# Preparing the next batch beside a batch's scan, and zeroing DRAM scratch beside the lookups

## The chip, the core and the metric

The kernel runs on one core of one Trainium2 chip. The metric is the time of one execution on the device in microseconds (us). A core has five engines that run their own instruction queues in order: TensorE (PE, matmuls, with its weight loads as PEld), VectorE (DVE), ScalarE (ACT), GpSimd (POOL), and SyncE (SP), which here only issues DMAs. POOL issues DMAs too. The on-chip memories are SBUF and PSUM; tables, partial sums and some intermediate results live in DRAM.

## What is computed

Four stages follow each other on an activation `x` of 4 batches x 512 tokens x 512 columns, each added to `x`:

```python
x = x + _L0_xattn_ref(_layernorm(x, axis=-1), fside_BxS2xS2_0, ctx_1024)
x = x + _L0_ffn_ref(_layernorm(x, axis=-1), L0_ffn_lut, L0_ffn_gate_idx, L0_ffn_up_idx, L0_ffn_down_idx)
x = x + _L1_xattn_ref(ctx_1024, _layernorm(x, axis=-1), L1_xattn_in_proj_w, L1_xattn_conv_w, ...)
x = x + _L1_ffn_ref(_layernorm(x, axis=-1), L1_ffn_gate_w, L1_ffn_w_gate, L1_ffn_w_up, L1_ffn_w_down)
```

The first is a pair of int8-quantized linears with a SiLU between them. The second is a gated FFN whose weights are looked up in a table of 16 values. The fourth is a mixture of 32 experts with the top 8 for each token. The change is about the third, a selective scan whose only link to `x` is the gate at its end:

```python
x = jnp.einsum('bld,ed->bel', hidden_states, in_proj_w)       # hidden_states is ctx_1024
xc = jax.lax.conv_general_dilated(x, conv_w, ...)             # 4 taps along the tokens
x = silu(xc + conv_b[None, :, None])                          # "u" in the kernel
x_dbl = jnp.einsum('bdl,ed->bel', x, x_proj_w)
dt_low, Bm, Cm = jnp.split(x_dbl, [dt_rank, dt_rank + d_state], axis=1)
dt = jax.nn.softplus(jnp.einsum('brl,dr->bdl', dt_low, dt_proj_w) + dt_proj_b[None, :, None])
...
state = state * jnp.exp(d[..., None] * A) + (d * u)[..., None] * b[:, None, :]   # for each token
y = jnp.einsum('bdn,bn->bd', state, c)
...
y = y + D[None, :, None] * x
y = y * silu(z)                                               # z is the layernorm of the running x
```

The convolution, the projection and the softplus need only the context, not the running `x`.

## The kernel before

The kernel is a list of Python generators. Each `yield` ends a step; `weave` interleaves the steps of several generators in proportion to weights, and that gives the order of the program. A scheduler then places the instructions on each engine's queue by that order and by when it reckons their inputs to be ready. Tiles come from pools; tiles with one tag share `bufs` buffers, so a new tile waits for the users of an old one.

- **Lookups** (to about 325 us). `smooth_quant` of the four batches is woven with `lut_weights`, which turns 27 groups of indices into FFN weights. The index loads go through SP (line 320) into two buffers `ix`.
- **Set-up.** `scan_weights` (line 400) loads the scan's weights. `routing_constants` (line 614) makes the router's constants, and zeroes what the experts need in DRAM: the first row of the two tables of normalized rows `xln` (line 644), 16 slot tables (line 669) and two sums of 4.5 MB each (line 671), all through SP.
- **Per batch, `scan` (line 478).** First a preparation: the context `cT` is loaded (line 484), four matmul groups `pi` (line 489), a convolution of three VectorE steps each (line 500), a SiLU into `u`, the projection `px` (line 510), which goes to DRAM as `xdbl` and comes back spread as `BC`, then the softplus. Its four slices `pd` (line 527) are done in two halves of two: Abs (533), max (534), Exp (537), three VectorE steps (539 to 541), then Ln for both halves (544), an add (545) and a product with `u` on POOL (546). The results, `dt` and `dt*u`, go to DRAM as `dts` through SP (line 549).
- Then the **scan proper**: 64 units a batch. Each loads 8 rows of `dts`, repeated 16 times over the partitions (512 KB, line 561), into half of a `pair` buffer. There are three pairs, and they share their tag with the softplus tiles. ScalarE takes exp into a PSUM bank `st` of tag "d" (line 566), POOL multiplies by B (568), VectorE runs the recurrence (569) and multiplies by C (571), and TensorE sums the states of four units at a time (578).
- Woven with the scan: the FFN of a batch, `lut_ffn`, 28 steps, and, from the second batch on, `route` of the batch before. The **gate** of the batch before (line 593) stands ahead of them; it uses a layernorm of a whole batch in a buffer `sz`, and PSUM tag "d".
- **After the last scan**: its gate and route, woven with the first 8 experts on the tokens of batches 0 and 1, and then all other expert work, which starts with reading the slot tables back.

PSUM in this part has tag "t" with 2 banks (transposes, the FFN's output, the router), "m" with 2 (FFN hidden), "y" with 1 (scan output) and "d" with 3.

Of the kernel before, what the change touches and what calls it, by code (L numbers as in the profile page):

```python
# [16 lines left out]
F32 = mybir.dt.float32  # L17
# [10 lines left out]
P = 128  # L28
# [31 lines left out]
class Kernel:  # L60
# [339 lines left out]
    def scan_weights(self, mp):  # L400
# [20 lines left out]
        self.dts = self.dram.tile([NB, HID, 2, S], F32, name="dts")  # L421

# [55 lines left out]
    def scan(self, mp, b):  # L478


        nc, t = self.nc, self.t
        conv_b, dt_b, skip = (self.vecs[:, i, :] for i in range(3))
        cT = mp.tile([P, DC // P, S], F32, tag="BC", name="cT", bufs=1)
        nc.sync.dma_start(out=cT, in_=t["ctxT"][b].rearrange("(k p) l -> p k l", p=P))
        u = mp.tile([P, KH, S], F32, tag="u", name="u", bufs=1)
        for e in range(KH):
            pi = self.bank("d", "pi")
# [19 lines left out]
        px = self.bank("d", "px")  # L507
# [3 lines left out]
        xd = mp.tile([nx, S], F32, tag="sc", name="xd", bufs=6)  # L511
        nc.scalar.copy(xd, px[:nx, :])
        nc.sync.dma_start(out=self.xdbl[b].rearrange("g n l -> (g n) l"), in_=xd)

        BC = mp.tile([P, 2, S], F32, tag="BC", name="BC", bufs=1)
# [4 lines left out]

        dts = []
        lost_ = mp.tile([P, KH, S], F32, tag="sz", name="lost", bufs=1)
        for e in range(KH):
            pd = self.bank("d", "pd")
            nc.tensor.matmul(
                pd, lhsT=self.dt_w[:, e * P : (e + 1) * P], rhs=xd[:RANK, :], start=True, stop=True
            )
            if e % 2 == 0:  # L530
                dts.append(mp.tile([P, 2, 2, S], F32, tag="dts", name="dt", bufs=3))
            d = dts[-1][:, e % 2]
            nc.scalar.activation(d[:, 1, :], pd, AF.Abs, bias=dt_b[:, e : e + 1])
            nc.vector.tensor_scalar(d[:, 0, :], pd, dt_b[:, e : e + 1], 0.0, ALU.add, ALU.max)
        for h, d in enumerate(dts):
            dt, w = d[:, :, 0, :], d[:, :, 1, :]
            nc.scalar.activation(w, w, AF.Exp, scale=-1.0)
            lost = lost_[:, 2 * h : 2 * h + 2, :]
            nc.vector.tensor_scalar(lost, w, 1.0, -1.0, ALU.add, ALU.add)
            nc.vector.tensor_tensor(lost, w, lost, ALU.subtract)  # L540
            nc.vector.tensor_tensor(dt, dt, lost, ALU.add)
        for h, d in enumerate(dts):
            dt, w = d[:, :, 0, :], d[:, :, 1, :]
            nc.scalar.activation(w, w, AF.Ln, bias=1.0)
            nc.vector.tensor_tensor(dt, dt, w, ALU.add)
            nc.gpsimd.tensor_tensor(w, dt, u[:, 2 * h : 2 * h + 2, :], ALU.mult)
            for i in range(2):
                e = 2 * h + i
                nc.sync.dma_start(out=self.dts[b, e * P : (e + 1) * P], in_=d[:, i])

        yield
        for e in range(KH):
            py = self.bank("y", f"py{e}")
            for v in range(4):
                scs = []
                for j in range(4):
                    if j % 2 == 0:
                        pair = mp.tile([P, 2, 2, S], F32, tag="dts", name="pair", bufs=3)
                    r0 = e * P + 32 * j + CPT * v
                    d = pair[:, j % 2]  # L560
# [30 lines left out]
        self.scanned = u  # L591

    def gate(self, mp, b):
# [3 lines left out]
        sz = mp.tile([P, TPB, HID], F32, tag="sz", name="sz", bufs=1)  # L597
        self.layernorm(sz, xb, TPB)
        for e in range(KH):
            th = mp.tile([P, S], F32, tag="sc", name="th", bufs=6)  # L600
            nc.scalar.activation(th, sz[:, e, :], AF.Tanh, scale=0.5)
            nc.vector.scalar_tensor_tensor(sz[:, e, :], th, 1.0, sz[:, e, :], ALU.add, ALU.mult)
            y = self.scanned[:, e, :]
            nc.vector.scalar_tensor_tensor(y, sz[:, e, :], 0.5, y, ALU.mult, ALU.mult)
            pt = self.bank("d", "pt_y")
# [574 lines left out]
```

## Time and profile before

| What | us |
|---|---|
| Median of 3 runs | 2057.48 (2054.28 to 2057.83) |
| The profiled execution | 2077.79 |
| Its span, first to last instruction | 2075.9 |
| PE busy | 1699.9 (82%) |
| DVE busy | 1216.7 (59%) |
| POOL busy | 975.7 (47%) |
| ACT busy | 673.6 (32%) |

The shares are means over parts with different limits. Roughly: 0 to 325 us lookups and quantized linears; 325 to 430 set-up, preparation of batch 0 and half of its FFN; 430 to 1199 the four scans; then experts to the end, where PE is busy nearly all the time from 1400 to 2000. The table of stretches that the prediction shows gives for each stretch its length, the busy time of each engine with the number of instructions in brackets, the TensorE clock granted, the busy share of the DMA engines (1 is full) and the GB/s moved. A line of the list of waits reads: engine, instruction's output and line, what it waited for, total us, times, longest us. A line of the timeline reads: start and length in us, engine, line, operation, output and inputs, number of instructions merged, and in brackets the engine's idle time before with what ended it. "SPq" is SP's issue of a DMA, not its transfer.

### The profile page before, as it was taken

To read this page: it belongs to the slowest core of one execution; us is meant where nothing else is said; L and a number is where in the kernel's file an instruction comes from. 1 tells how busy PE (TensorE), PEld (TensorE's weight loads), DVE (VectorE), ACT (ScalarE), POOL (GpSimd) and SP (SyncE) were. 2 spreads that over 40 slices of the span, in tenths; PEclk is the share of its full clock that TensorE was granted. 3 is DMA by queue.
4 is the path that set the end of the run, shared out by engine and by line. 5 is a ranking of instruction groups with operands and counts; after the bars stand their busy time and mean duration, and the time that the engine had idled before them with its cause. 6 is when DMAs were issued, how large, how long until landed. Compare 5 with 4: busy or idle time off the path is not lost. (4 is left out here: it accounts for less than half of the span.)

```text
span 2075.9 us, 24233 instructions
## 1 busy us (share of the span) xinstructions
PE 1699.9 (82%) x8385; PEld 996.7 (48%) x8385; DVE 1216.7 (59%) x2098; ACT 673.6 (32%) x1291; POOL 975.7 (47%) x844
## 2 busy tenths in 40 slices
PE   4777768978688779877987578679999999999980
PEld 2444337454344445544554244355556556566540
DVE  6777753479998888989888753122232223233232
ACT  1554342323453335333533332112222222222210
POOL 3111011055516771687168836635555555655431
PEclk9999978989898989998999689879999999999995
DMA  8421105099929972997299976648888877887756
GB/s 263 118 100 56 62 19 210 33 236 237 215 104 252 250 179 94 248 257 178 73 246 241 248 191 148 132 124 184 178 173 183 183 179 158 187 167 159 149 127 181
DMA packets 193207, 348.94 MB, mean 168 GB/s; under 512 B 46210, under 2 KB 92770, under 8 KB 193076
## 3 DMA queue, kind: packets, MB, share of 16 engines
q1 hardware_dynamic: 151332, 262.97, 47.2%
q0 software_dynamic: 41744, 84.34, 22.0%
q8 instruction: 68, 1.11, 0.2%
q14 instruction: 63, 0.52, 0.1%
HBM read 278.12 MB, written 77.57 MB: 171 GB/s over the span
## 5 line engine op out<-in xcount | busy, mean ns | idle before, releaser
L925 PE MATMUL pg<-exT,egu 128*128 128x320 f32 (+1 forms) x1536 | 408.2, 423 | 17.9 <-DVE eh L943 6.1
L968 POOL DMA_INDIRECT sums<-ey,to x168 | 261.0, 1554 | 283.3 <-DMA sums<-ey,to 128.5
L568 POOL TENSOR_TENSOR dBu<-pair,BC 128x512 f32<-128x512 f32 x256 | 326.8, 1279 | 134.5 <-DMA pair<-dts 116.4
L925 PEld LDWEIGHTS pg<-exT,egu 128*128 128x128 f32 x1536 | 291.6, 193 | 140.0 <-issue 44.7
L569 DVE TENSOR_TENSOR_SCAN st<-st,dBu 128x512 f32<-128x512 f32 x256 | 312.3, 1225 | 61.0 <-POOL dBu L568 49.4
L566 ACT ACTIVATE st<-pair,A 128x512 f32<-128x512 f32 x256 | 176.3, 691 | 330.5 <-DMA pair<-dts 269.2
L372 PE MATMUL pgu<-xT,wg 128*128 128x256 f32 (+1 forms) x704 | 199.8, 427 | 36.8 <-DVE h L382 36.5
L900 POOL DMA_INDIRECT xg<-xln,tokens x168 | 162.0, 964 | 103.5 <-PE pt_g L913 39.0
L942 DVE SCALAR_TENSOR_TENSOR eh<-eh,pg 128x320 f32<-128x320 f32 (+5 forms) x144 | 61.1, 424 | 227.9 <-ACT eh L941 127.9
L372 PEld LDWEIGHTS pgu<-xT,wg 128*128 128x128 f32 (+1 forms) x704 | 140.8, 209 | 104.0 <-DVE h L382 57.9
L333 PE MATMUL pw<-oh,lut_t 128*32 128x344 bf16 (+1 forms) x2052 | 131.3, 376 | 71.7 <-DVE oh L327 71.5
L372 PE MATMUL pgu<-xT,wu 128*128 128x256 f32 (+1 forms) x704 | 181.6, 398 | 0.0
L388 PE MATMUL po_f<-wd,h 128*128 128x512 f32 (+1 forms) x352 | 171.3, 631 | 12.1 <-DVE h L382 11.3
L954 PE MATMUL po_e<-ed,eh 128*128 128x512 f32 (+1 forms) x336 | 170.8, 628 | 12.0 <-DVE eh L943 4.1
L571 DVE TENSOR_TENSOR sc<-st,BC 128x512 f32<-128x512 f32 x256 | 169.0, 677 | 1.5
L965 DVE TENSOR_SCALAR ey<-po_e,gates 128x512 f32<-128x512 f32 x64 | 45.8, 747 | 210.4 <-PE po_e L958 127.5
L967 ACT ACTIVATE ey<-po_e,gates 128x512 f32<-128x512 f32 (+1 forms) x104 | 68.8, 684 | 285.4 <-PE po_e L958 140.3
L372 PEld LDWEIGHTS pgu<-xT,wu 128*128 128x128 f32 (+1 forms) x704 | 136.5, 198 | 40.5 <-issue 19.1
L578 PE MATMUL py<-sc,sum_states 128*32 128x512 f32 x512 | 80.7, 706 | 84.3 <-DVE sc L571 83.9
L796 POOL DMA_INDIRECT table<-i_tok,to x128 | 127.0, 992 | 38.9 <-issue 23.1
L333 PEld LDWEIGHTS <-lut_t 128*32 128x32 bf16 x2052 | 59.6, 105 | 124.8 <-issue 85.1
L388 PEld LDWEIGHTS po_f<-wd,h 128*128 128x128 f32 (+1 forms) x352 | 68.3, 201 | 98.8 <-issue 78.0
(266 smaller groups left out, 2011.1 us busy)
## 6 DMA issues: line engine op xcount, KB each, us to landing
pair<-dts SPq DMA_DIRECT2D x256, 512.0 KB
egu<-in_w_gate SPq DMA_DIRECT2D x40, 384.0 KB
ix<-idx_b SPq DMA_DIRECT2D x16, 688.0 KB
egu<-in_w_up SPq DMA_DIRECT2D x40, 256.0 KB
ed<-in_w_down SPq DMA_DIRECT2D x40, 256.0 KB
ed<-in_w_down SPq DMA_DIRECT2D x80, 128.0 KB
sums<-zero SPq DMA_DIRECT2D x2, 4608.0 KB
dts<-dt SPq DMA_DIRECT2D x16, 512.0 KB
```

The costliest lines, as they stand in the source:

```text
L333: nc.tensor.matmul(pt[i][32 * c : 32 * c + 32, :step], lhsT=self.lut_t[:, j, g, :], rhs=oh[:, c * n + i * step : c * n + (i + 1) * step], ...
L372: nc.tensor.matmul(pg[:m, j * W : (j + 1) * W], lhsT=w[:, k, c * P : c * P + m], rhs=xT[:, k, :], start=k == 0, stop=k == KH - 1,)
L388: nc.tensor.matmul(po, lhsT=h[:m, c, i * P : (i + 1) * P], rhs=self.wd[:m, c, :], start=c == 0, stop=c == NIC - 1,)
L566: nc.scalar.activation(st, d[:, 0, :], AF.Exp, scale=self.A[:, i : i + 1])
L568: nc.gpsimd.tensor_tensor(dBu, d[:, 1, :], BC[:, 0, :], ALU.mult)
L569: nc.vector.tensor_tensor_scan(st, st, dBu, 0.0, ALU.mult, ALU.add)
L571: nc.vector.tensor_tensor(sc, st, BC[:, 1, :], ALU.mult)
L796: scatter = nc.gpsimd.indirect_dma_start(out=tables[k % len(tables)], out_offset=bass.IndirectOffsetOnAxis(ap=to[:, i, k : k + 1], axis=0) ...
L900: nc.gpsimd.indirect_dma_start(out=xg[:m, :], out_offset=None, in_=xln, in_offset=bass.IndirectOffsetOnAxis(ap=tokens[:m, lo + j, col : co ...
L925: nc.tensor.matmul(pg[i][:, :hs], lhsT=w[:, k, i * P : (i + 1) * P], rhs=xT[:, k, z : z + hs], start=k == 0, stop=k == KH - 1,)
L954: nc.tensor.matmul(po[j][:m, :], lhsT=h[:, 0, b : b + m], rhs=wd[:, 0, :], start=True, stop=False)
L968: nc.gpsimd.indirect_dma_start(out=sums[j], out_offset=bass.IndirectOffsetOnAxis(ap=to[:m, lo + j, col : col + 1], axis=0), in_=y[:m, :], ...
```

## The change

It does the following.

- `scan` is split. `prepare` holds the convolution, the projection and the softplus, in nine steps; `scan` keeps the load of `BC` and the 64 units. `prepare` of batch 0 runs before the loop, woven with six FFN steps. `prepare` of batch b + 1 is woven with the scan of batch b. `u` gets two buffers.
- The softplus goes slice by slice, four times in a row, through one buffer `dt`: Abs, Relu, Exp and Ln on ScalarE. Its store to DRAM is issued by POOL instead of SP, and that of `xdbl` by ACT.
- The scan loads each unit into a tile `d` of its own, four buffers, in place of three pairs.
- The matmuls of the preparation and the gate's transposes use PSUM tag "t" in place of "d".
- The gate makes its layernorm row block by row block in scan buffers "sc". The router's `xn` has one buffer in place of two.
- Zeroing moves from `routing_constants` to a generator `scratch` that is woven with the lookups from step 36 on; each sum is zeroed by six stores in place of one, and every store is pinned behind what stands before it in SP's program. `routing_constants` comes after the first `prepare`.

```diff
-    def scan(self, mp, b):
+    def prepare(self, mp, b):
...
-        cT = mp.tile([P, DC // P, S], F32, tag="BC", name="cT", bufs=1)
+        cT = mp.tile([P, DC // P, S], F32, tag="c", name="cT", bufs=1)
...
-        u = mp.tile([P, KH, S], F32, tag="u", name="u", bufs=1)
+        u = self.u[b] = mp.tile([P, KH, S], F32, tag="u", name="u", bufs=2)
...
-            pi = self.bank("d", "pi")
+            pi = self.bank("t", "pi")
...
-        nc.sync.dma_start(out=self.xdbl[b].rearrange("g n l -> (g n) l"), in_=xd)
+        nc.scalar.dma_start(out=self.xdbl[b].rearrange("g n l -> (g n) l"), in_=xd)
+        yield
+        for e in range(KH):
+            pd = self.bank("t", "pd")
+            nc.tensor.matmul(
+                pd, lhsT=self.dt_w[:, e * P : (e + 1) * P], rhs=xd[:RANK, :], start=True, stop=True
+            )
+            d = mp.tile([P, 2, S], F32, tag="dt", name="dt", bufs=1)
+            dt, w = d[:, 0, :], d[:, 1, :]
+            nc.scalar.activation(w, pd, AF.Abs, bias=dt_b[:, e : e + 1])
+            nc.scalar.activation(dt, pd, AF.Relu, bias=dt_b[:, e : e + 1])
+            nc.scalar.activation(w, w, AF.Exp, scale=-1.0)
+            lost = mp.tile([P, DC // P, S], F32, tag="c", name="lost", bufs=1)[:, 0, :]
+            nc.vector.tensor_scalar(lost, w, 1.0, -1.0, ALU.add, ALU.add)
+            nc.vector.tensor_tensor(lost, w, lost, ALU.subtract)
+            nc.scalar.activation(w, w, AF.Ln, bias=1.0)
+            nc.vector.tensor_tensor(dt, dt, lost, ALU.add)
+            nc.vector.tensor_tensor(dt, dt, w, ALU.add)
+            nc.gpsimd.tensor_tensor(w, dt, u[:, e, :], ALU.mult)
+            nc.gpsimd.dma_start(out=self.dts[b, e * P : (e + 1) * P], in_=d)
+            yield
+
+    def scan(self, mp, b):
...
-                    if j % 2 == 0:
-                        pair = mp.tile([P, 2, 2, S], F32, tag="dts", name="pair", bufs=3)
...
-                    d = pair[:, j % 2]
+                    d = mp.tile([P, 2, S], F32, tag="d", name="d", bufs=4)
...
     def gate(self, mp, b):
...
-        sz = mp.tile([P, TPB, HID], F32, tag="sz", name="sz", bufs=1)
-        self.layernorm(sz, xb, TPB)
+        u = self.u[b]
         for e in range(KH):
...
+            sz = mp.tile([P, 1, S], F32, tag="sc", name="sz", bufs=6)
+            self.layernorm(sz, xb[:, e : e + 1, :], 1)
...
-            pt = self.bank("d", "pt_y")
+            pt = self.bank("t", "pt_y")
...
+    def scratch(self, c):
...
+        zero = c.tile([P, SLOTS], F32, name="zero")
+        nc.vector.memset(zero, 0.0)
...
+        yield from self.clear(zero, self.tables[0] + self.tables[1], SLOTS)
...
         for s in self.sums:
-            nc.sync.dma_start(
-                out=s.rearrange("(a p) d -> p a d", p=P),
-                in_=zero[:, :HID].unsqueeze(1).to_broadcast([P, NT + 2, HID]),
-            )
+            for a in range(0, NT + 2, 3):
+                z = nc.sync.dma_start(
+                    out=s.rearrange("(a p) d -> p a d", p=P)[:, a : a + 3, :],
+                    in_=zero[:, :HID].unsqueeze(1).to_broadcast([P, 3, HID]),
+                )
+                self.tc.keep_in_program_order(z)
+                yield
...
-            xn = rp.tile([P, 1, HID], F32, tag="xn", name="xn_r", bufs=2)
+            xn = rp.tile([P, 1, HID], F32, tag="xn", name="xn_r", bufs=1)
...
-                weave((sq, 30 * NB), (k.lut_weights(lp, k.jobs), 4 * len(k.jobs)))
+                lookups = k.lut_weights(lp, k.jobs)
+                weave((islice(sq, 40), 40), (islice(lookups, 36), 36))
+                weave((sq, 30 * NB - 40), (lookups, 4 * len(k.jobs) - 36), (k.scratch(lc), 4 * CHAINS))
...
+            weave((k.prepare(mp, 0), preps), (islice(ffn_, 6), 6))
             k.routing_constants(rp)
...
             for b in range(NB):
-                n = steps + (4 if b == 0 else 0)
+                n = steps - (2 if b == 0 else 0)
                 streams = [(k.scan(mp, b), units), (islice(ffn_, n), n)]
+                if b + 1 < NB:
+                    streams.append((k.prepare(mp, b + 1), preps))
```

## The prediction

> **What bounds the kernel now.** The cores view first: one core, span 2075.9 us; the profiled execution took 2077.8 us, 1.0% over the median of the runs, 2057.5 us. All sums below are made in that execution and carried to the median unchanged. Then the table of engine busy time by stretch. I cut it where the scan instruction (line 569) of each batch starts and stops; the same cut for that line alone gives 64 of them in each "scan" stretch and none in the four others.
>
> ```profile
> core 0: us, PE busy (x) PEld busy (x) DVE busy (x) ACT busy (x) POOL busy (x), PEclk, DMA share, GB/s
> 325.00:430.00 105.00, 99.60 (x350) 68.30 (x351) 44.69 (x106) 29.66 (x48) 9.79 (x18) 0.91 0.44 152
> 430.00:571.00 141.00, 104.42 (x408) 60.28 (x406) 129.98 (x170) 53.63 (x87) 82.20 (x68) 0.87 0.99 229
> 571.00:631.00 60.00, 52.33 (x186) 27.00 (x185) 54.06 (x117) 27.20 (x44) 11.13 (x10) 0.89 0.38 129
> 631.00:774.00 143.00, 111.77 (x457) 65.48 (x458) 127.87 (x171) 51.63 (x85) 112.54 (x98) 0.91 0.96 227
> 774.00:838.00 64.00, 61.28 (x232) 36.58 (x232) 54.16 (x126) 34.62 (x55) 11.99 (x11) 0.92 0.32 113
> 838.00:980.00 142.00, 109.98 (x448) 63.34 (x448) 130.29 (x171) 51.86 (x84) 112.41 (x98) 0.94 0.97 233
> 980.00:1046.00 66.00, 60.53 (x238) 37.14 (x239) 55.92 (x132) 35.12 (x56) 11.28 (x10) 0.92 0.30 98
> 1046.00:1199.00 153.00, 108.28 (x408) 57.88 (x406) 129.19 (x169) 50.84 (x90) 125.23 (x109) 0.84 1.04 245
> ```
>
> The reader should see two kinds of stretch. In a scan the 16 DMA engines are full (0.96 to 1.04): 64 loads in 141 us is 2.2 us a load. VectorE is then 84 to 92% busy. In a gap of 60 to 66 us the DMA falls to a third, yet VectorE stays at 85 to 90%. So a gap isn't empty: most of it is gate, routing, convolution and softplus on VectorE. Moving work out of a gap therefore doesn't save the gap; it saves the idle parts of VectorE, and no more. That is the main point of the forecast.
>
> Next the list of waits and the timeline, for where the idle time sits.
>
> ```profile
> ACT st L566 <- DMA pair<-dts: 269.2, 189, 12.4
> POOL dBu L568 <- DMA pair<-dts: 116.4, 132, 7.0
> ...
> 339.05 6.77 SPq L671 DMA_DIRECT2D sums<-zero  x2
> 345.86 11.53 SPq L484 DMA_DIRECT2D cT<-in_ctxT  x1
> ...
> 382.48 7.03 PE L489 MATMUL pi<-cT,in_w 128*128 128x512 f32 x16
> ...
> 417.46 5.39 SPq L549 DMA_DIRECT2D dts<-dt  x4
> ...
> 429.08 0.69 ACT L566 ACTIVATE st<-pair,A 128x512 f32<-128x512 f32 x1 [3.91 <-DMA pair<-dts]
> ...
> 628.98 0.69 ACT L566 ACTIVATE st<-pair,A 128x512 f32<-128x512 f32 x1 [12.39 <-DMA pair<-dts]
> ```
>
> ScalarE's wait for loads is the DMA bound of the scans. At the start, the load of batch 0's context stands behind 9 MB of zeros on SP's queue, its convolution begins at 382.5, and the scan at 430.5. TensorE isn't idle there: it runs half a batch of FFN first. And between two batches ScalarE waits 12.4 us for the first tile to go out to DRAM and come back; VectorE has other work for 9.8 of the 12 us from 620, so even this is mostly covered.
>
> **What the Trainium skill says.** "ScalarE: Activation LUTs", What ACT_TABLE_LOAD costs: a switch of set costs a 1283 ns load, and a drain as well. The trace has the load at 1283 ns: six at line 544 (Ln), and reloads for the next exp or tanh. "SBUF — State Buffer", SBUF: two separate sides: a DMA issued by GpSimd can wait for its descriptors while VectorE holds the shared port. The trace shows only a possible echo, line 546 on POOL taking 2341 to 3502 ns for one form. "DMA: Bandwidth & Descriptors", Issuing engines are not separate DMA queues: a store issued by GpSimd shares the same 16 engines, so moving it buys no bandwidth. No run here shows it; I charge the store its full slot.
>
> **The change part by part.**
>
> *Zeros.* 16 table and 12 sums stores move from 331-346 us into the lookups. DMA share there is 0.06 to 0.44 after the first 40 us, so 9.4 MB find room. SP is charged 7.4 + 1.4 us for tables and 6.8 us for sums, all behind or ahead of index loads, of which SP spends 136 us waiting for buffers. A store of 0.77 MB ahead of an index load delays it by about 3 us (at 260 GB/s); most of these have a spare buffer. Bounds: 0 to +10 us; taken +3.
>
> *Start of batch 0.* The scan weights are issued by 330.4, the context load follows and lands near 334. The old chain then gives: convolution matmul to u done 15 us (382.5 to 397.8), u to xd 2, first softplus slice Abs 0.7, Relu 0.7, Exp 0.6, two VectorE steps 1.1, table load and Ln 1.9, one add 0.7, POOL product about 1.5, so some 9 us with semaphores; then dts store to first scan 13 us (417.5 to 430.5), plus about 1 us because GpSimd issues it. 334 + 15 + 2 + 9 + 14 = 374; taken 376. Only the first of four slices stands before the scan; with one dt buffer the others follow at some 14 us each, and the scan needs one every 35 us. The scan starts 54 us earlier, but this isn't a saving of 54 us: of the 44.7 us of VectorE work before 430, about 25 come before 376 (FFN of six steps, convolution, one slice, constants), so 20 move behind it.
>
> *VectorE work from 376 to the end of scan 3.* From 430 to 1199 the table sums to 681.5 us. Add the 20. Take off the max at line 534 in three batches, 12 x 0.74 = 9, which becomes a ScalarE Relu. Add four layernorms of one row block for one of four (line 103 and 106, six more small ones a batch, 0.16 each) and four half-length softplus steps for two: about 4. Sum 697 us.
>
> *What it is divided by.* This is the choice that decides. The old mean from 430 to 1199 is 681.5/769 = 0.886. Its 88 us of idle time are 62 in the four scans (11, 15, 12 and 24: length less busy), where the DMA is last, and 26 in the three gaps (6, 10 and 10), where chains through other engines are. Only these can be won. After the change each load has 697/256 = 2.7 us of VectorE work beside it instead of 2.0, so the 2.2 us of DMA is no longer last; the whole DMA work of that stretch, shares times lengths, is 637 us, 84% of what follows. I take 0.92, the best that a scan stretch shows, since instructions are queued in a fixed order and other engines are not slack: TensorE has about 660 us of busy time in it. 697/0.92 = 758, end of scan 3 at 1134 instead of 1202: -68. At 0.886 the end is 1163 (-39), at 0.97 it is 1095 (-107).
>
> *Edits hidden at first sight.* ScalarE gets Relu 0.69 x 16 and single Exp and Ln calls; with exp of the scan between slices, each Ln costs two loads, 16 x 2.6 = 41 us against about 15 now. It is 44% busy, and three st banks hold 3 x 1.9 = 5.7 us of VectorE work, which covers a pause of 3.2 us; without that cover 12 slices x 3 = 36 us. The matmuls of the preparation and of the gate move from the three banks "d" to the two banks "t", beside po_f, which holds one for 10 us at a time; the price is TensorE waiting, with 10% to spare, 0 to +15, in the divisor. POOL gets 16 stores of about 0.7 us (as for line 304): +11 on 469, hidden. The d buffers fall from three pairs to four singles: see the slower rival.
>
> *Behind the last scan.* Gate and route of batch 3 sit on the chain to the late experts: TensorE is busy only half of 1330 to 1372. The layernorm of the gate can't all run before the scan ends, as it now borrows scan buffers: +5. The one routing buffer xn instead of two makes each layernorm wait for its store: 3 steps grow from 3 us to about 5: +5. Bounds +2 to +20; taken +10.
>
> Sum: -68 + 3 + 10 = -55 us; 2057.5 - 55 = 2002.5.
>
> **The rivals.**
>
> *A. More overlap.* VectorE at 0.97: -107 + 10 = -97, 1960 us. For it: it is fed by several independent streams. Against: no stretch of 50 us in the trace is above 0.95.
>
> *B. New waits eat the periods.* Every preparation step stops the ScalarE or TensorE queue for a bank, for the single dt buffer or for Ln, and exp of the scan waits behind it. At 0.86 and a tail of +25: 697/0.86 = 810, end 1186, -16 + 28 = +12 at worst, with the cover half there about 2045 us.
>
> *C. The four d buffers (slower).* Place: SP's loads at the d tile. With three pairs a load takes 10 us from issue to use, the first alone 6.2 us. A buffer is then held 1.4 us until POOL is done, so four of them give one load per (6.2 + 1.4)/4 = 1.9 us at best, under the 2.2 of the DMA. If stores of dts, xln and kept stretch a load's trip, the ring becomes the bound. It decides from a cycle of (1202 - 376 - 13)/256 = 3.2 us a load, a trip of 11.3 us. At 12.2 us it is 3.4 us a load: 376 + 870 + 13 = 1259, +57, 2114 us; nearer the point, 2080. For it: such trips of 15 to 20 us do occur at the end of scan 3, when expert weights load. Against: with fewer loads in flight the own queue is shorter.
>
> **How the numbers follow.** Forecast 0.60 (1975 to 2030), A 0.12, B 0.14 (0.10 faster, 0.03 same, 0.01 slower), C 0.14. About 0.2%, 4 us, can be told from no change. Faster 0.60 + 0.12 + 0.10 = 0.82, same 0.03, slower 0.15. The range takes the forecast with its bounds (divisor, tail, zeros), nearly all of A and the better half of B: 1953 to 2046; C is left out. The likeliest case's own range is 1975 to 2030.
>
> **What would show it.** First scan instruction near 376; no stretch without scans of over 15 us between batches; VectorE 90% or more and DMA near 0.85 from there to the last scan near 1134; ACT table loads up to about 40; the late experts (line 925) about 55 us earlier, from their first matmul to their end as long as before. Wrong if the first scan stays after 400, if VectorE is below 0.87 there, if loads take over 11 us from issue to use, or if the lookups end after 335.

## The result

The changed kernel takes 2083.23 us (median of 4 executions, 2079.09 to 2087.18). The ratio to the kernel before is 1.0121, with a 95% interval of 1.0090 to 1.0153: slower by 1.2%, where 2.7% faster was forecast. The time lies outside the range, and the sign is wrong. The profiled execution took 2087.18 us. That is only 9 us more than the 2077.79 us of the profile before, because that profile caught a long execution: over all later runs the kernel before took 2042.81 to 2077.45 us. So sizes below are taken from ratios (1% is 20.6 us), and places from the traces; differences of places from the kernel before carry that error too.

### The profile after

The same table of stretches, cut at the first scan instruction of each batch. The gaps of 60 us and more without scans are gone. The last line is a part of the second.

```profile
core 0: us, PE busy (x) PEld busy (x) DVE busy (x) ACT busy (x) POOL busy (x), PEclk, DMA share, GB/s
325.00:375.00 50.00, 44.12 (x159) 29.08 (x160) 24.98 (x63) 24.32 (x37) 4.11 (x8) 0.90 0.26 70
375.00:563.00 188.00, 152.29 (x555) 84.76 (x553) 162.09 (x225) 92.23 (x143) 99.28 (x86) 0.91 0.84 207
563.00:781.00 218.00, 180.83 (x682) 107.79 (x679) 187.62 (x309) 94.17 (x152) 133.20 (x119) 0.88 0.74 188
781.00:999.00 218.00, 178.62 (x700) 103.46 (x698) 189.51 (x308) 94.67 (x154) 132.58 (x120) 0.92 0.74 184
999.00:1186.00 187.00, 143.29 (x598) 87.73 (x598) 160.34 (x275) 60.37 (x106) 125.25 (x112) 0.89 0.84 203
...
375.00:435.00 60.00, 39.42 (x120) 21.36 (x119) 42.97 (x59) 28.25 (x44) 27.41 (x26) 0.80 0.71 179
```

The first scan instruction came as forecast: it stands at 375 instead of 430. But after four of them the scan stands still for 27 us, from 382.8 to 410.1, while the last two softplus slices of batch 0 go through ScalarE and VectorE; VectorE is busy for 43 of the 60 us to 435. Between the batches no more than 11 us pass without a scan instruction. The DMA share is down to 0.74 to 0.84, also as forecast. Yet from the start on the four periods take 811 us, where scans and gaps took 769 before. VectorE is busy for 700 of them, which is 0.863 of the time and not 0.92. The last scan ends at 1185, 13 us earlier than before, not 68.

The waits of the changed kernel from 375 to 1186 (waiting engine, line, what it waited for; total us, times, longest):

```profile
ACT st L561 <- DVE sc L566: 219.8, 110, 10.4
...
ACT st L561 <- DMA d<-dts: 43.9, 33, 5.0
POOL dBu L563 <- DMA d<-dts: 42.3, 44, 7.5
...
ACT dt L525 <- DMA dts<-dt: 36.7, 7, 7.5
...
DVE lost L529 <- ACT dt L527: 27.4, 8, 5.4
DVE ln_off L106 <- POOL ln_rs L104: 23.1, 17, 4.4
...
DVE st L564 <- POOL dBu L563: 22.6, 16, 5.1
...
DVE st L564 <- ACT st L561: 9.5, 2, 8.1
```

and one line of the kernel before:

```profile
DVE st L569 <- POOL dBu L568: 49.4, 58, 5.5
```

Before, ScalarE waited 269 us for loads. Now it waits 44 us for loads, and 220 us for VectorE to free a PSUM bank. VectorE is last, as the forecast wanted, and still stands idle for 111 us of the stretch (before: 87 of 768). The line for L525 is new: ScalarE stops before the next slice until the store has emptied the single dt buffer. The lines of DVE show what was won and what was lost. VectorE's waits for POOL's product, behind which the loads stand, fell from 49.4 to 22.6 us. In their place it waits 27.4 us for the Exp of a softplus slice (line 529) and 23.1 us for POOL in the layernorms (line 106; 4.6 us before).

Behind the last scan another 22 us went: the late experts start 193.6 us after it (1185.3 to 1378.9), where it was 171.4 us (1198.1 to 1369.5).

### The profile page after: what moved, and what is told of

Same layout as the page of the kernel before. It is cut to its first block, busy times and chain, and to the rows that moved or that the text cites. A ratio compares the mean times of both kernels' runs of the same rounds, so it can differ in the third digit from the quotient of the medians.

```text
span 2085.4 us, 24364 instructions
## 1 busy us (share of the span) xinstructions
PE 1703.8 (82%) x8385; PEld 1003.2 (48%) x8385; DVE 1218.4 (58%) x2138; ACT 707.8 (34%) x1343; POOL 999.5 (48%) x880
## 5 line engine op out<-in xcount | busy, mean ns | idle before, releaser
L563 POOL TENSOR_TENSOR dBu<-d,BC 128x512 f32<-128x512 f32 x256 | 337.3, 1324 | 221.8 <-DVE st L564 108.9
L564 DVE TENSOR_TENSOR_SCAN st<-st,dBu 128x512 f32<-128x512 f32 x256 | 303.7, 1213 | 33.7 <-POOL dBu L563 22.6
L561 ACT ACTIVATE st<-d,A 128x512 f32<-128x512 f32 x256 | 173.8, 689 | 269.2 <-DVE sc L566 219.8
L372 PE MATMUL pgu<-xT,wg 128*128 128x256 f32 (+1 forms) x704 | 195.2, 422 | 41.5 <-DVE h L382 41.5
L372 PE MATMUL pgu<-xT,wu 128*128 128x256 f32 (+1 forms) x704 | 175.9, 390 | 0.0
```

Source lines behind the costliest of these rows:

```text
L372: nc.tensor.matmul(pg[:m, j * W : (j + 1) * W], lhsT=w[:, k, c * P : c * P + m], rhs=xT[:, k, :], start=k == 0, stop=k == KH - 1,)
L561: nc.scalar.activation(st, d[:, 0, :], AF.Exp, scale=self.A[:, i : i + 1])
L563: nc.gpsimd.tensor_tensor(dBu, d[:, 1, :], BC[:, 0, :], ALU.mult)
L564: nc.vector.tensor_tensor_scan(st, st, dBu, 0.0, ALU.mult, ALU.add)
```

## The experiments

Ratios are to the kernel before, timed beside each run. "Last scan" and "late experts" (their first matmul) are read from each run's trace, one execution each. Not all rows were timed on the same chip, so they are compared by their ratios.

| Run | Median us | Ratio (95% interval) | Last scan ends | Late experts start |
|---|---|---|---|---|
| changed kernel | 2083.23 | 1.0121 (1.0090 to 1.0153) | 1185.3 | 1378.9 |
| block | 2116.99 | 1.0263 (1.0220 to 1.0306) | 1223.2 | 1416.4 |
| zeros | 2021.41 | 0.9796 (0.9755 to 0.9837) | 1144.4 | 1322.2 |
| split | 2064.40 | 1.0021 (0.9996 to 1.0045) | 1169.8 | 1359.5 |
| tail | 2058.23 | 0.9987 (0.9968 to 1.0005) | 1184.4 | 1356.6 |
| inline | 2075.71 | 1.0134 (1.0102 to 1.0165) | 1189.5 | 1381.3 |
| inline6 | 2071.15 | 1.0094 (1.0066 to 1.0123) | 1182.3 | 1377.6 |
| both | 2036.34 | 0.9928 (0.9907 to 0.9949) | 1170.8 | 1338.8 |
| noln | 2049.49 | 0.9982 (0.9966 to 0.9998) | 1161.7 | 1351.6 |
| zeros_slice | 2040.31 | 0.9877 (0.9839 to 0.9915) | 1156.5 | 1333.7 |
| gate | 2077.09 | 1.0077 (1.0053 to 1.0101) | 1175.8 | 1368.4 |
| best | 2020.95 | 0.9808 (0.9777 to 0.9839) | 1152.7 | 1322.9 |
| all | 2034.82 | 0.9870 (0.9839 to 0.9901) | 1163.3 | 1332.5 |
| all_noln | 2032.86 | 0.9856 (0.9827 to 0.9886) | 1136.7 | 1317.8 |
| zeros_noln | 2028.43 | 0.9823 (0.9792 to 0.9854) | 1146.8 | 1330.1 |
| pair | 2055.21 | 0.9945 (0.9925 to 0.9965) | 1164.0 | 1346.5 |
| zeros_half | 1980.82 | 0.9637 (0.9607 to 0.9666) | 1108.4 | 1290.3 |
| all_half | 1998.27 | 0.9721 (0.9693 to 0.9750) | 1128.6 | 1302.5 |

### First theory: the weave gains nothing, and the tail loses

**zeros** is the kernel before with its zeroing moved, as the change has it, and nothing else:

```diff
...
-                weave((sq, 30 * NB), (k.lut_weights(lp, k.jobs), 4 * len(k.jobs)))
+                lookups = k.lut_weights(lp, k.jobs)
+                weave((islice(sq, 40), 40), (islice(lookups, 36), 36))
+                weave((sq, 30 * NB - 40), (lookups, 4 * len(k.jobs) - 36), (k.scratch(lc), 4 * CHAINS))
```

> The kernel before with one part of the change alone: the zeros are stored beside the lookups. The context of batch 0 no longer waits behind them on SP's queue. Theory 1: scan 0 starts some 20 us earlier (430 to about 410), half of that is given back as VectorE work that moves behind the start, the last scan ends 8 to 15 us earlier, time 2040 to 2050. Rival (the start is worth nothing, since FFN and VectorE work of the same amount must still be done): within 4 us of the kernel before.

Faster by 2.0% (the two medians alone, 2021.41 and 2059.39, give 1.8%): more than twice what was expected, and the largest single effect of the study. Its stretch from its first scan to its last:

```profile
core 0: us, PE busy (x) PEld busy (x) DVE busy (x) ACT busy (x) POOL busy (x), PEclk, DMA share, GB/s
380.00:1144.50 764.50, 630.94 (x2498) 371.04 (x2496) 681.51 (x1061) 303.79 (x500) 459.70 (x395) 0.92 0.82 203
```

The first scan moves from 430 to 380 with the preparation where it was, and all of it arrives at the last scan (1144.4 for 1198.1); no stop as in the changed kernel follows the start. VectorE's work from the first scan on is 681.5 us, the same as before from 430 on. So the early start, which the forecast gave to the change as a whole, comes from the zeros alone. What is left of the change then costs 1.0121 / 0.9796 = 1.033, some 67 us.

**block** and **inline** put the preparation of batches 1 to 3 back between the scans, with all else as changed:

```diff
 block:
-                if b + 1 < NB:
-                    streams.append((k.prepare(mp, b + 1), preps))
                 if b:
+                    run(k.prepare(mp, b))
                     run(k.gate(mp, b - 1))
 inline:
-                streams = [(k.scan(mp, b), units), (islice(ffn_, n), n)]
-                if b + 1 < NB:
-                    streams.append((k.prepare(mp, b + 1), preps))
+                streams = [(chain(k.prepare(mp, b), k.scan(mp, b)) if b else k.scan(mp, b), units + (preps if b else 0)), (islice(ffn_, n), n)]
```

> The changed kernel, but the preparations of batches 1 to 3 stand as blocks between the scans again; the early start of batch 0, the zeros beside the lookups and all buffers stay. Theory 1 (the woven preparation gains nothing, because VectorE's queue, which runs in order, is stopped by its short chains as long as the gaps cost before): the last scan ends within 10 us of the changed kernel's 1185, time within 12 us of 2083. Rival (the weave does what the forecast said and the loss lies elsewhere): three gaps come back, last scan ends at 1210 or later, time 2105 to 2125.

> The changed kernel, but the preparation of batches 1 to 3 stands in front of its own scan in one stream, as in the kernel before, so that FFN and routing steps fill the gap (in run block they did not). All buffers, forms and banks of the change stay. Theory 2 (the forms that the weave needed, single buffers, slice by slice softplus, shared bank and short layernorms, cost the 40 us that the scans grew over run zeros; the weave itself gives nearly as much as it takes): as slow as the changed kernel, last scan ends at 1180 or later, time 2075 to 2095. Rival (the weave itself costs them, by chains put between scan units): back to run zeros in the scans, last scan near 1150, and with the tail's loss of 22 us a time of 2040 to 2052.

Block came out where its rival said, at 2117 us. But it undoes more than the weave: in its three gaps VectorE is busy for 28 of 42 to 46 us, since no FFN step fills them, and the scans beside which they stand instead take 185 to 191 us. It said little about the weave. Inline has the order of the kernel before, with FFN steps in the gaps, and is as slow as the changed kernel: 1.0134 and 1.0121, intervals that nearly coincide. So the weave is not where the time went. On the buffers and forms of the change it neither gains nor loses, to within the intervals; the loss is there without it, and comes with the buffers and forms that were changed to make room for it.

### Second theory: the forms cost, one by one

**tail** changes two things for batch 3 alone: where the gate's transposes go, and a second buffer for the router.

```diff
-            pt = self.bank("t", "pt_y")
+            pt = self.bank("d" if b == NB - 1 else "t", "pt_y")
...
-            xn = rp.tile([P, 1, HID], F32, tag="xn", name="xn_r", bufs=1)
+            pool, tag = (self.mp, "xd") if b == NB - 1 and i % 2 else (rp, "xn")
+            xn = pool.tile([P, 1, HID], F32, tag=tag, name="xn_r", bufs=1)
```

> The changed kernel with two edits that act behind the last scan only: the transposes of the gate of batch 3 use PSUM tag d (free by then) instead of t, and the router of batch 3 has a second buffer for its normalized rows. Theory 1 (the 22 us that the stretch from the last scan to the late experts grew come from these two): late experts 10 to 18 us earlier, time 2065 to 2073. Rival (they come from the expert instructions that stand ahead in ScalarE's and POOL's queues): under 5 us, 2078 to 2086.

1.3% faster, some 28 us, where 10 to 18 were expected. The scans end where they did (1184.4 and 1185.3), and the late experts start 22 us earlier. First the timeline of the changed kernel, gate and router of batch 3 (start, length, engine, line, in brackets the idle time before):

```profile
1190.47 1.11 PE L603 MATMUL pt_y<-ident,u 128*128 128x128 f32 x4 [2.05 <-DVE ln_rs L103]
...
1215.35 0.66 PE L603 MATMUL pt_y<-ident,u 128*128 128x128 f32 x4
...
1235.21 0.81 ACT L108 ACTIVATE xn_r<-x,ln_off,ln_rs 128x512 f32<-128x512 f32 x1 [0.70 <-DMA xln<-xn_r]
```

Then the same in run tail:

```profile
1196.00 0.60 PE L603 MATMUL pt_y<-ident,u 128*128 128x128 f32 x4
...
1201.56 0.63 PE L603 MATMUL pt_y<-ident,u 128*128 128x128 f32 x4 [1.15 <-DVE u L599]
...
1207.71 1.76 ACT L108 ACTIVATE xn_r<-x,ln_off,ln_rs 128x512 f32<-128x512 f32 x2 [6.90 <-DVE ln_off L106]
```

Four transposed tiles are spread over 25 us in the changed kernel, between transposes and outputs of the first experts that use the same two banks; in run tail they are through in 6 us. The router then makes two rows' layernorms back to back, where it waited for the store of the row before: its four layernorms start within 8 us, and took 19. The last logits come out at 1224.7 instead of 1244.8, and the scatters and the late experts move up with them. The two edits were not run apart. In the traces some 13 of the 20 us are won before the first of the router's layernorms, where the banks act, and some 6 after it, where the buffer does.

**split** cuts a softplus slice into three woven steps, **noln** leaves the logarithm out (Identity in its place):

```diff
 split:
             nc.scalar.activation(w, w, AF.Exp, scale=-1.0)
+            yield
             lost = mp.tile([P, DC // P, S], F32, tag="c", name="lost", bufs=1)[:, 0, :]
...
             nc.vector.tensor_tensor(dt, dt, lost, ALU.add)
+            yield
             nc.vector.tensor_tensor(dt, dt, w, ALU.add)
 noln:
-            nc.scalar.activation(w, w, AF.Ln, bias=1.0)
+            nc.scalar.activation(w, w, AF.Identity, bias=1.0)
```

> The changed kernel with each softplus slice cut into three steps instead of one (a step ends after the Exp and after the first add), so that its VectorE instructions are woven in later than the ScalarE instructions they wait for. Theory 1: VectorE's wait for the Exp (27 us, line 529) falls by half or more, its idle time between 375 and the end of the last scan falls from 111 us to about 95, the last scan ends 10 to 20 us earlier, time 2063 to 2073. Rival (the idle time only changes its name, the bound being elsewhere): the wait at the slice falls but the sum stays at 105 to 115, time 2078 to 2088.

> The changed kernel with the logarithm of the softplus left out: Identity in its place, which reads and writes the same tile in the same time and needs no other table. Theory of the table loads (16 slices at two loads of 1.28 us each stop ScalarE, and VectorE behind it): last scan ends 15 us or more earlier, time 2055 to 2068. Rival (ScalarE has slack, it waits 220 us for free banks anyway): within 6 us of 2083.

Both gained, split 1.0% and noln 1.4%, each a little more than its theory asked. The groups of the changed kernel show the table loads, with which ScalarE changes its set of functions (busy us, mean ns, then idle time before and what ended it):

```profile
L531 ACT ACT_TABLE_LOAD x16 | 20.5, 1283 | 9.8 <-DVE lost L530 8.6 <-DVE ln_rs L103 1.1
...
L380 ACT ACT_TABLE_LOAD x8 | 10.3, 1283 | 0.1
L561 ACT ACT_TABLE_LOAD x8 | 10.3, 1283 | 2.0 <-DMA d<-dts 1.9
```

From 375 to the last scan the changed kernel loads tables 28 times, run zeros 8 times, run noln never. Twenty loads more are 26 us of ScalarE. Of the 28, 14 stand in front of a slice's Ln, and 14 in front of the exp of the scan or the tanh of the FFN that follows it, as the timeline of the changed kernel shows for one slice, with two lines of the next slice at its end:

```profile
702.08 0.62 ACT L527 ACTIVATE dt<-dt 128x512 f32<-128x512 f32 x1
...
705.11 0.69 ACT L561 ACTIVATE st<-d,A 128x512 f32<-128x512 f32 x1 [1.82 <-DVE sc L566]
...
706.35 1.28 ACT L531 ACT_TABLE_LOAD   x1 [0.55 <-DVE lost L530]
...
706.79 2.20 DVE L532 TENSOR_TENSOR dt<-dt,lost 128x512 f32<-128x512 f32 x1
707.17 1.27 POOL L563 TENSOR_TENSOR dBu<-d,BC 128x512 f32<-128x512 f32 x1
707.64 0.63 ACT L531 ACTIVATE dt<-dt 128x512 f32<-128x512 f32 x1
708.29 1.28 ACT L380 ACT_TABLE_LOAD   x1
...
722.80 0.69 ACT L525 ACTIVATE dt<-pd,vecs 128x512 f32<-128x512 f32 x1 [7.52 <-DMA dts<-dt]
...
724.62 0.43 DVE L529 TENSOR_SCALAR lost<-dt 128x512 f32<-128x512 f32 x1 [5.44 <-ACT dt L527]
```

ScalarE waits for VectorE (the bank of line 561), VectorE's queue holds the slice's steps, and these wait for ScalarE (27.4 us at line 529). Two queues that run in order wait for each other by turns. In run split the slice's wait falls from 27.4 to 8.0 us and VectorE's idle time from 111 to 94; in run noln they fall to 8.7 and 88.

The last two lines show a second cause that no run took out by itself: the single dt buffer. Seven of the eight waits at line 529, 27.0 of the 27.4 us, come straight after ScalarE stood at line 525 until the store had emptied that buffer. This stand falls from 36.7 us to 7.2 in run split and 9.8 in run noln. So both runs may gain by way of the buffer, and a second dt buffer with all the loads in place was not tried: what the loads cost and what the buffer costs isn't told apart.

Split and noln remove largely the same time: with split in place (run all below, which has other edits too), leaving out the logarithm gains 0.1% in the ratio, within the intervals.

**both** is tail and split together, **gate** computes the statistics of the four row blocks at once, **inline6** gives run inline six load buffers instead of four (the room comes from the second u buffer):

```diff
 gate:
+        rs, off = self.statistics(xb, TPB)
         for e in range(KH):
             sz = mp.tile([P, 1, S], F32, tag="sc", name="sz", bufs=6)
-            self.layernorm(sz, xb[:, e : e + 1, :], 1)
+            self.normalize(sz, xb[:, e : e + 1, :], rs[:, e : e + 1], off[:, e : e + 1])
 inline6:
-                    d = mp.tile([P, 2, S], F32, tag="d", name="d", bufs=4)
+                    d = mp.tile([P, 2, S], F32, tag="d", name="d", bufs=6)
```

> Runs split and tail in one kernel. If the two losses stand in different stretches and add up, 19 + 25 us come off the changed kernel: 2035 to 2043. If the one was only the other's shadow (both end at the same later bound): 2052 to 2060. Either way the rest over run zeros, some 18 us, would be what weaving costs still.

> The changed kernel, but the gate computes the statistics of its four row blocks in one go (one power on POOL instead of four), and still normalizes block by block in the scan's buffers. Theory 2: four of VectorE's waits for POOL a batch become one, the waits of line 106 fall from 23 us to about 12, last scan some 8 us earlier, time 2068 to 2078. Rival (these waits stand where VectorE would wait for something else): within 4 us of the changed kernel, a ratio of 1.010 to 1.014.

> Run inline with one u buffer instead of two, as its order allows, and six d buffers in their room instead of four. Theory of the ring (four load buffers are too few once the scan runs alone beside the DMA): 15 us or more faster than run inline, the wait for d in ScalarE and POOL falls. Rival (the ring is not the bound): within 6 us of run inline.

Tail and split nearly add up (0.9928, with an interval from 0.9907; 1.0121 less 1.3% and 1.0% is 0.989). Gate gains 0.4%, with intervals that just overlap, and its last scan ends 9.5 us earlier, as expected, though its waits for POOL at the layernorms fell only from 23.1 to 19.3 us, where about 12 was expected. So the gate's form explains little of these waits. Inline6 gains 0.4% over inline, with intervals that overlap, half of what its theory asked: the ring of four, the slower rival of the prediction, is at most a small part.

**zeros_slice** is the cross-check from the other side: run zeros, and the slice-by-slice softplus alone, in the old place and with the old buffers.

```diff
-        for h, d in enumerate(dts):
-            dt, w = d[:, :, 0, :], d[:, :, 1, :]
-            nc.scalar.activation(w, w, AF.Exp, scale=-1.0)
...
+            nc.scalar.activation(w, w, AF.Exp, scale=-1.0)
+            lost = lost_[:, e, :]
...
+            nc.scalar.activation(w, w, AF.Ln, bias=1.0)
```

> Run zeros with the softplus slice by slice, as the change has it (Abs, max, Exp, Ln of one slice before the next), in its old place between the scans and in its old buffers. Theory 2 (the form, not the weave, costs): every batch gets up to six more table loads of 1.28 us on ScalarE and shorter VectorE steps, in a stretch where the scan waits for the first slices anyway: 8 to 25 us slower than run zeros, a ratio to the kernel before of 0.984 to 0.992. Rival (the loads hurt only where the scan's exp stands behind them): within 4 us of run zeros.

0.9877 for 0.9796: the form costs some 0.8% with no weave and no single dt buffer, with intervals that just part.

### Is a repaired weave worth it?

**all** has split, tail and gate, and copies the gates of the first experts one step later; **best** is run zeros with the changed gate and the later copies for batch 3; **pair** is run all with one Ln for two slices. The last keeps the computation whole, with one half of the second slice in the context's buffer:

```diff
 best, all:
+            if xln is self.xln[0]:
+                nc.scalar.copy(gates[:m, j : j + 1], xg[:m, HID + e : HID + e + 1])
         yield
         half = len(blocks) // 2
 pair:
-            nc.scalar.activation(w, w, AF.Ln, bias=1.0)
+            nc.scalar.activation(d[:, :2, :], d[:, :2, :], AF.Ln, bias=1.0)
```

> The changed kernel with runs split, tail and gate together, and the copies as in run best. If all add up: 2036 - 8 - 5, 2020 to 2028, as fast as run zeros, so that the weave itself would be worth what the table loads and the ring still cost (some 30 us). If the waits at the gate were covered: 2030 to 2036, still behind run zeros.

> Run zeros with two edits behind its last scan: the gate of batch 3 normalizes row block by row block, as the change has it (the three others stay whole), and ScalarE copies the gates of the first eight experts one step later, so that the last exp of the scan doesn't stand behind a copy that waits for a gather. In the trace of run both the stretch from the last scan to the late experts is 168 us, in run zeros 178. If that comes from the gate's form: 8 to 12 us faster than run zeros, ratio 0.974 to 0.976; if it does not, the copies alone give 3 us.

> Run all with two slices of the softplus side by side, so that one Ln instruction does both (complete computation): 19 table loads in the program where run all has 35. To find the room, the projection and one half of the second slice live in the context's buffer, and the stores to DRAM are single halves (16 of 256 KB more packets of half the size). Theory 3: half of the loads' price comes back, 10 to 14 us faster than run all, ratio 0.980 to 0.983, level with run zeros. Rival (the chain through the one shared buffer gets longer, and VectorE waits for it): as run all, 0.985 to 0.990.

All reached 0.987, faster than the kernel before and 0.7% behind run zeros (0.6% behind best, which was timed beside it). So its edits didn't make the weave level with run zeros, as its first theory had it. Best missed its expectation and didn't gain on run zeros; the copies and the gate's form bring nothing there. Pair was slower than all by 0.8%, worse than both its theory and its rival: it has half the loads (14 in its scans for 28), and lost. That each pair holds the shared buffers longer is the likely reason, not a shown one.

**all_noln** and **zeros_noln** leave the logarithm out of both orders, so that the table loads can't decide:

> Run all with the logarithm of the softplus left out (Identity in its place, no table loads). Theory 3 (the weave in itself is worth some 20 us, and the table loads take it back): 20 to 30 us faster than run all, ratio 0.973 to 0.977, and 8 us or more faster than run zeros_noln. Rival (the weave is worth nothing even without its forms' price): within 5 us of run zeros_noln or slower.

> Run zeros with the logarithm left out in the same way. It has 8 table loads in its scans, in gaps, for 28 of the woven kernels: 0 to 8 us faster than run zeros, ratio 0.976 to 0.980.

The rival held: 0.9856 woven, 0.9823 not woven, overlapping intervals. Even without that price the weave isn't worth anything that these runs can measure. Zeros_noln missed its own expectation: without its logarithm run zeros is no faster (0.9823 for 0.9796, overlapping intervals), so the 8 loads in its scans cost nothing that can be measured. The last scan of all_noln, 27 us earlier than that of all in the table, is no counter-proof: its profile caught the fastest of six executions, 2020.34 us for a median of 2032.86.

**zeros_half** and **all_half** ask why. Two units share one load, so half the loads are left out.

```diff
+                    if j % 2 == 0:
                         d = mp.tile([P, 2, S], F32, tag="d", name="d", bufs=4)
```

> Run zeros with half of the scan's loads left out: two units share one load of 8 rows, so that every second unit computes on the wrong rows; the work of all engines stays. The forecast's premise (the idle time of VectorE in the scans, 62 us before, is the DMA's): scans shrink from 141 us to 130 or less, time 30 us or more below run zeros, ratio 0.965 or less. Theory 4 (the DMA ends last in the scans, but VectorE's other waits stand right behind it): waits for the load go, VectorE's idle time falls by less than 25 us, ratio 0.970 to 0.979.

> Run all with half of the scan's loads left out in the same way. Loads are not last in the woven order: within 8 us of run all, ratio 0.983 to 0.989. If they are (the ring of four), 0.980 or less.

Unwoven, half the loads are worth 1.6%: the forecast's premise, that the DMA holds up the scans, is true, and theory 4 fell. But the woven order gains 1.5% as well, as the second alternative of its expectation had it: loads still hold it up. Its waits from 380 to 1130, run all:

```profile
ACT st L572 <- DVE sc L577: 205.7, 99, 8.6
...
ACT st L572 <- DMA d<-dts: 57.5, 43, 3.9
POOL dBu L574 <- DMA d<-dts: 51.6, 50, 3.0
```

In run all_half the two waits for loads are gone from the list, and VectorE's idle time falls from 93 to 71 us. So at a DMA share of 0.81 loads still come late, and the weave didn't win what it was for. Whether that is the ring of four buffers, bunched loads or both wasn't tried. Nor are the loads all: with half of them gone VectorE is busy for 686 of 758 us in run all_half, 0.906, and for 678 of 730 in run zeros_half, 0.929.

## Why the prediction was wrong

- **Start of batch 0, "taken 376".** Right for the first instruction: 375.3. "Only the first of four slices stands before the scan" was wrong: two more stood before the fifth scan instruction, a stop of 27 us that run zeros (1 us) and run inline (7 us) don't have. And in run zeros VectorE's work behind the start didn't grow by the 20 us that were to move there (681.5 us in both). At an unchanged 0.886 the forecast's start was worth 39 us; run zeros measured 2.0%, 42 us. The step stood in the forecast under the wrong name: it needs nothing of the weave.
- **Zeros beside the lookups, "taken +3".** Hidden: the last step of the quantized linears (line 240) ends at 323.0 (before: 326.6).
- **VectorE work, 697 us.** Measured 699, by luck as a sum. Of the FFN nine more steps each of lines 381 and 382 came behind the start (83 for 74), some 7 us and not 20. In place of the rest, instructions got longer: 38 of them, over 0.2 us longer than the shortest of their kind while a POOL product of line 563 ran, are 31.5 us longer in all; in run zeros 6 such are 4.8 us. The view of line 106 in the changed kernel (shortest, median, longest ns):

```profile
L106 DVE SCALAR_TENSOR_TENSOR ln_off<-ln_mv,ln_rs x31: 142/160/2310, 475.7 to 1161.5; 128x1 f32<-128x1 f32 x26, 128x2 f32<-128x2 f32 x5
```

and in run zeros:

```profile
L106 DVE SCALAR_TENSOR_TENSOR ln_off<-ln_mv,ln_rs x20: 152/160/164, 523.8 to 972.2; 128x1 f32<-128x1 f32 x12, 128x2 f32<-128x2 f32 x5, 128x4 f32<-128x4 f32 x3
```

  The Trainium skill states a cause ("SBUF — State Buffer", Who interferes with whom): a VectorE instruction with two SBUF inputs contends with a GpSimd instruction that reads SBUF, and the later of the two waits for the whole other. The trace agrees where it was looked at closely: four of the long ones of line 106, 1.21 to 1.22 us for 0.16, end 15 to 20 ns after a product that began 53 to 62 ns before them. The prediction cited the same page and looked only at DMA descriptors. In the old order much of this VectorE work stands in the gaps, where POOL is busy for 11 to 12 of 60 to 66 us. Run inline, which has the old order, shows 15 such instructions, 14.1 us, but more idle time (126 us); the two nearly cancel.
- **"What it is divided by … I take 0.92."** This step failed, and with it the sign. Measured: 0.863, under the 0.87 that the forecast itself named as a sign of being wrong; the old mean was 0.886, run zeros has 0.891. The premise, that the DMA's idle time can be won, was half right (run zeros_half). The changed kernel won 27 us of it (the waits for POOL's product, 49.4 to 22.6 us; 32.5 in run inline, without the weave) and kept the rest (run all_half). Against that stand the new waits, 27.4 us for the slice's Exp and 18 us more for POOL in the layernorms. Run inline has them too, 27.0 us at line 529 and 20.4 us at line 106, so they came with the forms and not with the weave. And 0.92 was out of reach: the woven order stays below it even with half its loads left out (0.906). In the forecast's sum 0.863 for 0.92 is 50 of the 80 us between 2002.5 and 2083, and the tail 12 to 18. The rest of some 15 us can't be placed in the traces, since the profile before was itself a long execution.
- **"Edits hidden at first sight."** Here the forms were priced at nothing, and this is a good part of why the divisor failed. The term that failed is "three st banks hold 3 x 1.9 = 5.7 us of VectorE work, which covers a pause of 3.2 us". The banks did cover what they were said to cover: ScalarE was so far ahead that it waited 220 us for a freed bank, and VectorE waited for the exp of the scan (line 561) only twice, 9.5 us. What no bank covers is the slice's own Exp, for which VectorE stood 27.4 us at line 529, behind table loads and the single dt buffer. Without the cover 36 us were named; run noln measured 1.4%, 29 us. The single dt buffer was priced only for batch 0, and there as slack.
- **Tail, "Bounds +2 to +20; taken +10".** Right in kind, too small: 22 us in the traces, 1.3% or 28 us in run tail. The single xn buffer was named; the two PSUM banks shared with the first experts were put to the scans' account, with 0 to +15.
- **Rivals.** B, "new waits eat the periods", named the divisor of 0.86 and the end at 1186, which is what came, within a microsecond at the scan's end, and among its waits the single dt buffer. It had 0.14, of it 0.01 for slower, and its worst sum was +12 us, where 25 came. C, the ring of four, isn't the main cause: the longest waits for a load are 5.0 us on ScalarE and 7.5 us on POOL, and six buffers gain 0.4% (tried in the order of run inline only).

Settled by runs: the gain (zeros, 2.0%), the tail (1.3%), the slice-wise softplus with its loads and its buffer (1.0 to 1.4% woven, some 0.8% not), and that with the buffers and forms of the change weave or not makes no difference (inline). That a repaired weave gains nothing either is less sure: all and zeros, and the same two without the logarithm, differ in their forms too. Not settled: the gate (0.4%, overlapping intervals), what table loads and dt buffer cost each, and how the last 0.7% between run all and run zeros divides. The blocked VectorE time (30 us in run all) would do, but was read from the traces and not tried by itself.

## What to carry to other kernels

Price the room that a reordering needs (smaller rings, a single buffer, a shared bank, short pieces of a long step) as parts of the change in their own right; here the changed kernel is 3.3% behind the version without them, and the reordering gave nothing. Ask of a cover which wait it covers: three banks covered the scan's exp, and VectorE stood for another instruction of the same queue. When a change has several parts, ask what each part would do alone: the zeroing stores moved out of the context's way were the whole gain, and run zeros, at 0.98 of the time before, is the version to keep. Idle time of an engine between other engines' waits was not free to take here: the short chains woven into its in-order queue brought waits of their own.

## What the runs showed of the hardware

- A table load cost ScalarE 1283 ns and little more: in the slice above Ln ends at 708.27 and the tanh starts at 709.58, 1.31 us later. The Trainium skill ("ScalarE: Activation LUTs", What ACT_TABLE_LOAD costs) adds a drain of about 1.38 us; this trace has no room for it.
- TensorE's granted clock goes with the time of the kernel: 0.894 to 0.902 in the executions of block, 0.905 to 0.909 in those of the changed kernel, 0.920 to 0.925 in run zeros. Which causes which isn't shown.
- A kernel with the same instructions moved by up to 1.4% between executions on one chip and 1.7% over all (the kernel before, 2046.26 to 2074.20 and 2042.81 to 2077.45 us), and a profile catches one of them. A profile and a median can differ by more than the effect that is looked for.
